# A fused four-layer kernel: which eighths of the queries keep their probabilities stationary, turned queries exchanged in pairs of chunks, and image copies issued in another stage

## The chip, the core and the metric

The kernel runs on one core of one Trainium2 chip. The metric is the device time of one execution in microseconds (us), the median of several runs. The core has a matrix engine (TensorE, PE in the profile; its weight loads are PEld), a vector engine (VectorE, DVE), an activation engine (ScalarE, ACT), a general engine (GpSimd, POOL) and an engine that only issues transfers and waits (SyncE, SP). Each of them takes its instructions in the order of the program. Data lies in 128 partitions of on-chip memory (SBUF); products are summed in eight banks (PSUM) of 512 float32 a partition. Transfers (DMA) run on 16 DMA engines, whichever queue issues them.

## The reference

Four images x of 256 channels and 64 x 64 pixels, all in float32, go through four residual layers, each on the group-normalised input (32 groups). Cut to what matters here:

```python
# layer 0: convolution 3x3, group norm, ReLU, then softmax attention over all 4096 pixels
xs  = relu(group_norm(conv3x3(_gn(x)), 8 groups))
f   = einsum('bnc,bcm->bnm', theta(xs), phi(xs))        # 4096 x 4096 logits an image
y   = einsum('bnm,bmc->bnc', softmax(f, axis=-1), g(xs))
x   = x + group_norm(conv1x1(y)) * 0.1 + xs

# layer 1: linear attention, 4 heads of 32
q, k, v = split(conv1x1(rmsnorm(_gn(x))))
q = softmax(q, over the 32 of a head);  k = softmax(k, over pixels)
context = einsum('bhdn,bhen->bhde', k, v)
x = x + rmsnorm(conv1x1(einsum('bhde,bhdn->bhen', context, q * scale)))

# layer 2: a 3x3 depthwise and a 1x1 kernel generated from the pooled image
x = x + conv1x1(depthwise3x3(_gn(x), dk), pk) + bias

# layer 3: a 1x1 kernel mixed of four experts
x = x + einsum('boc,bchw->bohw', w_mixed, _gn(x))
```

## The kernel before

**Two streams of work in one program.** The order of every engine's instructions is written out by hand. The softmax attention of batch b (`attend`) is a generator that advances by *steps*. Beside it runs a *chain* (`Chain`) of the other layers' work: layers 0's end, 1, 2 and 3 of batch b-1 (`tail`), and then the convolution of batch b+1 (`convolve`). `run` (L2271) takes a step of the chain and then one of the attention, in turns. The chain yields numbers: `yield n` lets n times `rate` steps of attention pass before its next instructions are emitted, and `yield None` exactly one. The rate is 0.785 beside batches 1 and 2 and 1.14 beside batch 3 (L2297, L2306). So a time in the program is a place in the sequence of steps, and where the chain's work comes late, the attention behind it in the same queue waits too.

**Attention.** The 4096 queries of a batch are eight *eighths* q of 512 (`NQ`), and an eighth is 16 steps m of 256 keys (`NM`); a batch has 128 steps. A step (L1207 on) issues the logits of the next step, two products of 512 columns into two banks `pf` and their exponentials by ScalarE into one tile `pr` (L1105, L1106), and then multiplies this step's probabilities with g, in one of two ways. *Moving* (L1221): g is the stationary operand, the 512 probabilities stream through, and the result `py` has channels in the partitions; the sum of the probabilities is made by VectorE, one addition of 128 x 1024 into `tot` a step (L1225, L1227). *Stationary* (L1218): 128 probabilities at a time are the stationary operand and g with a column of ones, 129 columns, streams through, so that PE makes the sum too; eight short products a step instead of two long ones. `across(q)` (L1201) chooses: stationary for q7 of every batch, and in batches 1 and 2 for every q from `TURNED` = 2 on.

**The end of an eighth** is a generator that gets one turn in each following step. For a stationary eighth, `ended` (L1166): VectorE copies the sums out of `py`, takes the reciprocal and scales; one step later PE turns the result (`ps_yt`), one more later it projects it (`ps_wy`). For a moving eighth, `ended_by_dram` (L1127): VectorE joins the halves of `tot` into `inv`, which goes to DRAM (`sum_d`, SyncE); one step later the *gather* `inv<-sum_d` (L1138, ScalarE's queue) reads it back turned, in pieces of 16 bytes; six steps after that VectorE reduces it (`r_inv`, L1142), the reciprocals go to DRAM (`rec_d`) and come back to all partitions, VectorE multiplies (`yq`), and PE projects (`ps_wy`) some 14 steps after the eighth's end.

**Linear attention in the tail** (L1520 to L1561) goes over eight chunks c of 512 pixels. A chunk is normalised (`normed`, into `xg`), turned in blocks of 32 by VectorE (`corners`), written to DRAM by four DMAs (`sent`, `turned_d`) and read back with pixels in the partitions (`fetched`), two chunks ahead of its use. ScalarE and GpSimd make the lengths (`lengths`, `rinv`), VectorE scales (`unit`). Then PE multiplies (`ps_qk`), ScalarE takes the exponentials (`qk_of`), VectorE normalises q, and a chunk later PE adds to the context (`ps_ctx`). The queries themselves are turned by the same exchange: `q_corners` (L1415), four DMAs `q_sent` of 64 KB into `q_d` and one `q_fetched` into `qT`. All of these DMAs are on SyncE. For c = 0, 2, 4 and 6 `copy_x` (L1542) also issues two DMAs of 512 KB from DRAM to DRAM there, which copy the image of batch b+2 into `xs_d`, where the layer's result is later added up; it does so in the tails that run beside attention 1 and 2.

The `outputs` of layer 1 go through a third exchange, `z_sent` and `z_fetched` through `z_d`, into the image by `z_added` with statistics (L1702 to L1723). At its end stands a chain of small steps: the statistics of the last chunk (`mv`), a product `pm`, small VectorE operations, a product `pv` (`group_finish`, L400), after which layer 2 begins.

**The depthwise stage** (`in_order`, L1920) goes over eight parts n (four chunks of 1024 pixels by two halves of the channels): ScalarE makes the centre tap, VectorE adds the eight others, one instruction of about 128 x 1024 a tap, and PE multiplies with the generated kernel (`ps_pw`). The convolution of the next batch follows, with filters of 256 KB loaded by SyncE.

**Buffers.** Tiles named by `k4` (4 KB a partition) share nine places: `pr`, `tot`, `wt`, `xg`, `qk`, `z`, `dw` and others. `k2` tiles have four places; `q_turn` is one of them before the change. A tile's instruction waits until the former tile in its place has been read for the last time.

Of the kernel before, what the change touches and what calls it, by code (L numbers as in the profile page):

```python
# [8 lines left out]
F32 = mybir.dt.float32  # L9
# [4 lines left out]
P = 128  # L14
# [3 lines left out]
CH = 1024  # L18
# [6 lines left out]
NQ = N // 512  # L25
# [11 lines left out]
TX1, MX1 = 4, 2  # L37
IX1 = HW // MX1
RW = MX * (IX + 1)
TURNED = 2  # L40
TW = 4 * (NH * 32 + 1)
US_A_STEP = 4.35
EASED = 0.68
# [61 lines left out]
def conv_preact_fast(ctx: ExitStack, tc: tile.TileContext, guard, in_range, x, wc, wtpg, ww, wqkv, wout, w1cat, wd2,  # L105
# [3 lines left out]
    nc = tc.nc  # L109
    B = x.shape[0]  # L110
# [9 lines left out]
    def k4(name):  # L120
        return k4_wide(name)[:, 0:CH]
# [3 lines left out]
    def k2(name):  # L125
        return wk.tile([P, 512], F32, tag="k2", name=name, bufs=4)
# [31 lines left out]
    qT = x_cols[:, 0, :]  # L158
# [101 lines left out]
    rows_d = tc.dram_tile([TY, P, NH, 3, NH * P], F32, name="rows_d")  # L260
    filters = tc.dram_tile([TY, P, TX - 2, NH, NH * P], F32, name="filters")
    turned_d = tc.dram_tile([NQ, 4, 32, 4, 4 * (NH * 32 + 1)], F32, name="turned_d")
    q_d = tc.dram_tile([NQ, 4, 32, 4, P], F32, name="q_d")
    z_d = tc.dram_tile([NQ, 4, 32, 4, NH * P], F32, name="z_d")
    taps = wc_s.rearrange("p h (i j) o -> p h i (j o)", i=3)

# [514 lines left out]
    def copy_x(b, part=None):  # L781
        for h in range(NH):
            cols = slice(0, N) if part is None else bass.ts(part, CH)
            nc.sync.dma_start(out=xs_d[b, h, :, cols], in_=x[b, bass.ts(h, P), cols])
# [287 lines left out]
    def attend(b):  # L1072
# [127 lines left out]

        def across(q):  # L1201

            return q == NQ - 1 or 0 < b < B - 1 and q >= TURNED

        xc = None
        logits(0)
        for i in range(NQ * NM):  # L1207
            q, m = divmod(i, NM)
# [147 lines left out]
    def linear_attention(w, b, big, qT, k4, st, sh, sums):  # L1356
# [14 lines left out]
        NC = N // 512  # L1371
# [20 lines left out]
        def sent(c, s):  # L1392
            for a in range(4):
                nc.sync.dma_start(out=turned_d[c, :, :, a, :].rearrange("c e n -> e c n"),
                                  in_=s[bass.ts(a, 32), :].rearrange("p (c n) -> p c n", c=4))
# [16 lines left out]
            for j in range(4):  # L1412
                nc.vector.tensor_scalar(x[:, :, j, 0:NH * 32], x[:, :, j, 0:NH * 32], rinv[:, j:j + 1], None, ALU.mult)

        def q_corners(qk):  # L1415
            s = k2("q_turn")
            nc.vector.transpose(s.rearrange("p (a j e) -> p a j e", a=4, j=4),
                                qk[:, :, 0:HID].rearrange("p j (a r) -> p a j r", a=4))
            return s

        def q_sent(c, s):
            for k in range(4):
                nc.sync.dma_start(out=q_d[c, :, :, k, :].rearrange("a r n -> r a n"),
                                  in_=s[bass.ts(k, 32), :].rearrange("p (a n) -> p a n", a=4))

        def q_fetched(c):
            nc.sync.dma_start(out=qT[:, bass.ts(c, 512)], in_=q_d[c].rearrange("a r c n -> (a r) (c n)"))

        def turned(xg):

# [30 lines left out]
        def qk_of(xg, rinv, first=()):  # L1461


            qk = k4("qk").rearrange("p (j o) -> p j o", j=4)
            for j in range(4):
                ps = first[j] if j < len(first) else product(xg, j)
                nc.scalar.activation(qk[:, j, :], ps[:, 0:2 * HID], AF.Exp, scale=rinv[:, j:j + 1])
                yield 0.125

            q = qk[:, :, 0:HID].rearrange("p j (g d) -> p j g d", d=HD)  # L1470
            qs = sp.tile([P, 4, HEADS], F32, name="qs", bufs=3)
            nc.vector.tensor_reduce(qs, q, AX.X, ALU.add)
            nc.vector.reciprocal(qs, qs)
            tt(q, q, qs.unsqueeze(3).to_broadcast([P, 4, HEADS, HD]), ALU.mult)
            return qk
# [12 lines left out]
        if alone:  # L1488
            w.fill(1)
            warm(3)  # L1490
            w.settle()
            xg, first = normed(0), ()
            rinv, banks = turned(xg)
            first = [product(xg, j) for j in range(2)]
            next(sums)
            xt = tokens(rinv, banks)
            yield 1
            last = None
            for c in range(NC):
                if c + 1 < NC:  # L1500
                    ahead = normed(c + 1)
                next(sums, None)
                if c == 2:
                    checks.append(counted())
                if c in (2, 4, 5):
                    next(checks[0])
                yield 0.5
                this = (yield from qk_of(xg, rinv, first)), xt
                first = ()
                if c + 1 < NC:  # L1510
                    xg = ahead
                    rinv, banks = turned(xg)
                if last is not None:
                    context(c - 1, *last)
                if c + 1 < NC:
                    xt = tokens(rinv, banks)
                last = this
            yield 1
            context(NC - 1, *last)
        else:  # L1520
            w.settle()
            nc.gpsimd.memset(quarters[3].rearrange("p (k o) -> p k o", k=16)[:, :, NH * 32:TW // 4], 1.0)
            xgs = {0: normed(0)}
            s = corners(xgs[0])
            yield 0.5
            sent(0, s)
            xgs[1] = normed(1)
            s = corners(xgs[1])
            yield 0.5
            xs = {0: fetched(0)}  # L1530
            sent(1, s)
            yield 1
            rinv = lengths(xs[0])
            last, turn = None, None
            for c in range(NC):
                if c + 1 < NC:
                    xs[c + 1] = fetched(c + 1)
                if c + 2 < NC:
                    xgs[c + 2] = normed(c + 2)
                    s = corners(xgs[c + 2])  # L1540
                unit(xs[c], rinv)
                if b + 2 < B and c % 2 == 0:  # L1542
                    copy_x(b + 2, c // 2)
                yield 0.5
                if turn is not None:
                    q_sent(c - 1, turn)
                if c + 2 < NC:
                    sent(c + 2, s)
                qk = yield from qk_of(xgs.pop(c), rinv)
                turn = q_corners(qk)  # L1550
                if c > 0:
                    q_fetched(c - 1)
                if last is not None:
                    context(c - 1, *last)
                if c + 1 < NC:
                    rinv = lengths(xs[c + 1])
                last = qk, xs.pop(c)
            q_sent(NC - 1, turn)
            yield 1
            q_fetched(NC - 1)  # L1560
            context(NC - 1, *last)  # L1561
        w.fill(1)
        rk = sp.tile([P, 1], F32, name="rk", bufs=1)
# [138 lines left out]
        s, zts = None, {}  # L1702
        for c in range(NC):
# [9 lines left out]
            s = z_corners(scaled(*zb))  # L1713
# [2 lines left out]
                w.fill(1)  # L1716
            yield 0.7
        z_sent(NC - 1, s)
        yield 0.5
        zts[NC - 1] = z_fetched(NC - 1)  # L1720
        z_added(NC - 2, zts.pop(NC - 2))
        yield 1.2
        z_added(NC - 1, zts.pop(NC - 1))  # L1723
        if b + 2 < B:
            nc.gpsimd.memset(ra[:, :, :, 0:1], 0.0)
# [39 lines left out]
    def generated(w, b, big, k4, st, sh, diag):  # L1765
# [55 lines left out]
        for c in range(N // 512):  # L1821
            if c < NC3:
                hidden(c)
            h, q = c % 2, c // 2
# [38 lines left out]
        def centre(i):  # L1863
            c, h = PARTS[i]
            t = k4("dw")
            k = h * 9 + 4
            nc.scalar.activation(t.rearrange("p (y x) -> p y x", x=HW), xin[:, h, bass.ts(c, rows), :], AF.Copy, scale=dk[:, k:k + 1])  # L1867
            return t
# [31 lines left out]
        def taps(i, some=TAPS, over=slice(0, CH // HW)):  # L1900

            c, h = PARTS[i]
            dst = dw[i].rearrange("p (y x) -> p y x", x=HW)[:, over, :]
            for ty, tx in some:
                dx = tx - 1
                x0, x1 = max(0, -dx), min(HW, HW - dx)
                k = h * 9 + 3 * ty + tx
                y = c * rows + ty
                stt(dst[:, :, x0:x1], xp[:, h, y + over.start:y + over.stop, x0 + dx:x1 + dx], dk[:, k:k + 1],
                    dst[:, :, x0:x1], ALU.mult, ALU.add)  # L1910
                yield 0.66
# [8 lines left out]
        def in_order(mine):  # L1920

            dw[mine[0]] = centre(mine[0])
            slices = [load_wp2(0), load_wp2(1)]
            for n, i in enumerate(mine):
                if n + 1 < len(mine):
                    dw[mine[n + 1]] = centre(mine[n + 1])
                for wait in taps(i):
                    yield wait * (EASED if n > 1 and b < B - 2 else 1)
                if n == 0:
                    for j in range(R):  # L1930
                        mix_kernel(slices, [j])
                        if j % 2 == 1 and j // 2 + 2 < R // 2:
                            slices.append(load_wp2(j // 2 + 2))
                        yield 0.35
                c, h = PARTS[i]
                if h == NH - 1:
                    d = [dw[2 * c + h] for h in range(NH)]
                    for s in range(2):
                        w.later(1 + s, lambda c=c, s=s, d=d: pointwise(c, s, d))
            yield 2  # L1940
            yield from w.pending()
# [950 lines left out]
```

## Time and profile before

| | |
|---|---|
| median of 3 runs | 2997.34 us (2995.27 to 2999.57) |
| time of the profiled execution | 2996.91 us |
| its span, first to last instruction | 2995.0 us |
| mean granted TensorE clock | 0.989 |
| first convolution and projections, until attention begins | 181 us |
| attention of batch 0, with the convolution of batch 1 and the projections | 181 to 744 us |
| batch 1 | 744 to 1477 us |
| batch 2 | 1477 to 2210 us |
| batch 3, and the last tail alone | 2210 to 2995 us |

The batches' borders are the starts of their first `pf` products. Batches 1 and 2 are the ones that the change of the eighths and of the copies concerns; their tails belong to the images of batches 0 and 1. Beside the attention of batch 3 runs the tail of batch 2, with neither.

How to read the profile's rows: a window row gives start and end, the length, then for each engine its busy time with the number of instructions in parentheses, the granted clock as a share, the share of the DMA engines' time in use, and GB/s. A row of waits says which instruction of which engine stood idle for whom: the total, how many times, and the longest. A timeline row gives start, length, engine and line, operation, the tile written and those read, how many in a row, and in brackets the idle time before it and what ended that. A product in float32 is listed as two records, so four `pf` records are the two products of a step.

### The profile page before, as it was taken

What the parts mean: (1) busy time and instruction counts of PE and PEld (TensorE: products, weight loads), DVE (VectorE), ACT (ScalarE), POOL (GpSimd) and SP (SyncE); (2) the same over time, 40 slices, a digit from 0 to 9 for tenths busy, and PEclk for the clock granted to TensorE, in tenths of its full rate; (3) what the DMA queues carried; (4) which work ended last, traced back from release to release, by engine and by line L of the source; (5) the groups of instructions that cost most, each with busy time, mean ns of one, the idle gap of its engine ahead of it and who ended that gap; (6) DMA issues with size and microseconds to landing.
All of it is one profiled execution on the core that took longest, in us unless ns stands there. A gap on an engine that the chain in (4) does not pass through costs nothing. (4 is left out here: it accounts for less than half of the span.)

```text
span 2995.0 us, 31153 instructions
## 1 busy us (share of the span) xinstructions
PE 2885.3 (96%) x11158; PEld 1734.3 (58%) x11158; DVE 1849.4 (62%) x2939; ACT 1341.5 (45%) x2720; POOL 189.8 (6%) x218
## 2 busy tenths in 40 slices
PE   7999999999987999999998899999999999999999
PEld 3554555566554666777555466677755644446744
DVE  8737667751656672686265585377536587783585
ACT  2234333435544543324564544422555555433674
POOL 0000000001001000000101000000000110000143
PEclk9999999999999999999999999999999999999999
DMA  5235543224565121110566502211165553225112
GB/s 226 76 84 123 65 74 68 39 32 99 169 150 134 46 78 64 53 57 32 123 191 135 113 29 78 74 50 64 32 159 122 98 126 63 25 32 135 48 65 77
DMA packets 423140, 262.71 MB, mean 88 GB/s; under 512 B 311425, under 2 KB 358273, under 8 KB 419457
## 3 DMA queue, kind: packets, MB, share of 16 engines
q1 hardware_dynamic: 123168, 239.14, 24.7%
q10 hardware_dynamic: 295200, 4.72, 7.8%
q0 software_dynamic: 4608, 16.78, 3.6%
q8 instruction: 90, 1.47, 0.2%
q14 instruction: 74, 0.60, 0.1%
HBM read 162.84 MB, written 114.53 MB: 93 GB/s over the span
## 5 line engine op out<-in xcount | busy, mean ns | idle before, releaser
L1106 ACT ACTIVATE pr<-pf 128x512 f32<-128x512 f32 x1024 | 599.1, 596 | 903.0 <-PE pf L1105 880.7
L1105 PE MATMUL pf<-tpg 128*128 128x512 f32 x2048 | 972.9, 597 | 3.9 <-ACT pr L1106 2.2
L1105 PEld LDWEIGHTS pf<-tpg 128*128 128x128 f32 x2048 | 376.5, 191 | 370.4 <-issue 339.4
L1221 PE MATMUL py<-pr,tpg 128*128 128x512 f32 x1152 | 543.7, 594 | 2.3 <-ACT pr L1106 2.3
L1218 PEld LDWEIGHTS py<-tpg,pr 128*128 128x128 f32 x3584 | 436.4, 192 | 109.1 <-issue 100.8
L1218 PE MATMUL py<-tpg,pr 128*128 128x129 f32 x3584 | 437.5, 275 | 2.4 <-ACT pr L1106 2.4
L1221 PEld LDWEIGHTS py<-pr,tpg 128*128 128x128 f32 x1152 | 219.1, 190 | 280.5 <-issue 263.7
L138 DVE TENSOR_TENSOR tot<-tot,pr 128x1024 f32<-128x1024 f32 x252 | 306.8, 1217 | 94.7 <-ACT pr L1106 94.1
L141 DVE SCALAR_TENSOR_TENSOR dw<-xp,dk,dw 128x1008 f32<-128x1008 f32 x192 | 242.2, 1269 | 7.3 <-ACT dw L1867 3.7
L706 PE MATMUL ps_conv<-v,u 128*128 128x256 f32 x864 | 195.7, 379 | 6.4 <-DVE v L138 3.6
L706 PEld LDWEIGHTS ps_conv<-v,u 128*128 128x128 f32 x864 | 161.5, 190 | 35.8 <-issue 11.5
L233 POOL TENSOR_TENSOR rstd<-rstd,half 128x2 f32<-128x2 f32 x24 | 17.7, 736 | 1933.9 <-DVE rstd L431 1789.7
L1457 PE MATMUL ps_qk<-wqkv_s,xg 128*128 128x256 f32 x496 | 116.6, 386 | 8.0 <-ACT pr L1106 7.4
L1029 PE MATMUL ps_tp<-big,wtpg_s 128*128 128x512 f32 x256 | 116.8, 595 | 4.0 <-ACT big L805 4.0
L138 DVE TENSOR_TENSOR tpg<-ps_g,bg_s 128x512 f32<-128x512 f32 x32 | 22.1, 691 | 155.7 <-PE ps_g L1034 155.7
L1457 PEld LDWEIGHTS ps_qk<-wqkv_s,xg 128*128 128x128 f32 x496 | 95.4, 194 | 32.1 <-ACT pr L1106 9.0
L141 DVE SCALAR_TENSOR_TENSOR sums<-ps_conv,sums 128x512 f32<-128x512 f32 x72 | 49.7, 690 | 90.6 <-PE ps_conv L706 84.9
L1875 PE MATMUL ps_pw<-dw,pk 128*128 128x512 f32 x192 | 86.3, 592 | 0.0
L1171 DVE COPY total<-py 128x2 f32<-128x2 f32 x28 | 4.5, 159 | 127.7 <-PE py L1218 127.7
L1029 PEld LDWEIGHTS ps_tp<-big,wtpg_s 128*128 128x128 f32 x256 | 45.9, 190 | 53.4 <-issue 42.1
L1030 ACT ACTIVATE tpg<-ps_tp,btp_s 128x512 f32<-128x512 f32 x64 | 44.0, 687 | 70.9 <-PE ps_tp L1029 70.9
L1034 PEld LDWEIGHTS ps_g<-wtpg_s,big 128*128 128x128 f32 x512 | 62.2, 192 | 15.3 <-issue 15.3
(486 smaller groups left out, 3284.4 us busy)
## 6 DMA issues: line engine op xcount, KB each, us to landing
u<-filters SPq DMA_DIRECT2D x72, 256.0 KB, 2.5
xp<-in_x_dram SPq DMA_DIRECT2D x16, 1024.0 KB, 8.4
xs_d<-big POOLq DMA_DIRECT2D x32, 512.0 KB, 6.1
wy_d<-wt SPq DMA_DIRECT2D x32, 512.0 KB, 3.0
wy<-wy_d SPq DMA_DIRECT2D x32, 512.0 KB, 5.0
out_dram<-res SPq DMA_DIRECT2D x64, 256.0 KB, 2.0
turned_d<-rt SPq DMA_DIRECT2D x96, 130.0 KB, 2.7
xs_d<-in_x_dram SPq DMA_DIRECT2D x24, 512.0 KB, 6.6
```

The costliest lines, as they stand in the source:

```text
L138: nc.vector.tensor_tensor(o, a, b, op)
L141: nc.vector.scalar_tensor_tensor(o, a, s, b, op0, op1)
L706: nc.tensor.matmul(ps[:, bass.ts(oh, IY * IX)], u[i][:, h, bass.ts(oh, P)], v[:, i, bass.ts(h, IY * IX)], start=(h == 0), stop=(h == NH - 1))
L1029: nc.tensor.matmul(ps, wtpg_s[:, h, k, :], big[:, h, cols], start=(h == 0), stop=(h == NH - 1))
L1030: nc.scalar.activation(tpg[:, k, cols], ps, AF.Identity, bias=btp_s[:, k:k + 1])
L1034: nc.tensor.matmul(ps[:, j, :], big[:, h, bass.ts(4 * c + j, P)], wtpg_s[:, h, 2, :], start=(h == 0), stop=(h == NH - 1))
L1105: nc.tensor.matmul(pf, phi[:, bass.ts(2 * m + s, P)], theta[:, bass.ts(q, 512)], start=True, stop=True)
L1106: nc.scalar.activation(pr[:, bass.ts(s, 512)], pf, AF.Exp)
L1218: nc.tensor.matmul(py[t // 2][:, t % 2, :], probs[i][:, s * 512 + t * P:s * 512 + (t + 1) * P], g[:, 2 * m + s, :], start=(begin and t % 2 ...
L1221: nc.tensor.matmul(py, g[:, 2 * m + s, 0:P], probs[i][:, bass.ts(s, 512)], start=begin, stop=end)
L1457: nc.tensor.matmul(ps[:, 0:2 * HID], xg[:, h, bass.ts(j, P)], wqkv_s[:, h, 0:2 * HID], start=(h == 0), stop=(h == NH - 1))
L1875: nc.tensor.matmul(ps, pk[:, h * NH * P + oh * P:h * NH * P + (oh + 1) * P], dw[h][:, bass.ts(s, 512)], start=(h == 0), stop=(h == NH - 1))
```

## The change

`TURNED` becomes a list of eighths, (0, 1, 3, 5, 6): in batches 1 and 2 the eighths q0 and q1 become stationary, and q2 and q4 moving. q7 stays stationary, batches 0 and 3 keep their choice.

The turned queries are exchanged in pairs of chunks. `q_turn` is now a `k4` tile for two chunks; after two chunks four DMAs of 128 KB write them to `q_d`, in a layout in which the pair's columns lie together for each partition, and one DMA reads 1024 columns back. In the chunk's order `sent(c + 2)` now stands ahead of `q_sent`, a pair is sent in the even chunk after it, and fetched in the odd one, ahead of `qk_of`.

`copy_x` leaves linear attention and is issued in the depthwise stage, at parts n = 2 to 5, one quarter of the image each.

Three yields change: after the last chunk `yield 1` becomes 0.3 ahead of the last `q_sent` and 0.7 after it; at the end of the z exchange 0.5 becomes 0.7, and 1.2 becomes 1.6.

```diff
-TURNED = 2
+TURNED = (0, 1, 3, 5, 6)
...
-    q_d = tc.dram_tile([NQ, 4, 32, 4, P], F32, name="q_d")
+    q_d = tc.dram_tile([NQ // 2, 4, 32, 2, 4, P], F32, name="q_d")
...
-            return q == NQ - 1 or 0 < b < B - 1 and q >= TURNED
+            return q == NQ - 1 or 0 < b < B - 1 and q in TURNED
...
-        def q_corners(qk):
-            s = k2("q_turn")
-            nc.vector.transpose(s.rearrange("p (a j e) -> p a j e", a=4, j=4),
+        def q_corners(c, qk, s):
+            nc.vector.transpose(s[:, bass.ts(c % 2, 512)].rearrange("p (a j e) -> p a j e", a=4, j=4),
                                 qk[:, :, 0:HID].rearrange("p j (a r) -> p a j r", a=4))
-            return s
-
-        def q_sent(c, s):
+
+        def q_sent(i, s):
             for k in range(4):
-                nc.sync.dma_start(out=q_d[c, :, :, k, :].rearrange("a r n -> r a n"),
-                                  in_=s[bass.ts(k, 32), :].rearrange("p (a n) -> p a n", a=4))
-
-        def q_fetched(c):
-            nc.sync.dma_start(out=qT[:, bass.ts(c, 512)], in_=q_d[c].rearrange("a r c n -> (a r) (c n)"))
+                nc.sync.dma_start(out=q_d[i, :, :, :, k, :].rearrange("a r i n -> r i a n"),
+                                  in_=s[bass.ts(k, 32), :].rearrange("p (i a n) -> p i a n", i=2, a=4))
+
+        def q_fetched(i):
+            nc.sync.dma_start(out=qT[:, bass.ts(i, CH)], in_=q_d[i].rearrange("a r i c n -> (a r) (i c n)"))
...
                 unit(xs[c], rinv)
-                if b + 2 < B and c % 2 == 0:
-                    copy_x(b + 2, c // 2)
                 yield 0.5
-                if turn is not None:
-                    q_sent(c - 1, turn)
                 if c + 2 < NC:
                     sent(c + 2, s)
+                if c % 2 == 0:
+                    if c > 0:
+                        q_sent(c // 2 - 1, turn)
+                    turn = k4("q_turn")
+                elif c > 1:
+                    q_fetched(c // 2 - 1)
                 qk = yield from qk_of(xgs.pop(c), rinv)
-                turn = q_corners(qk)
-                if c > 0:
-                    q_fetched(c - 1)
+                q_corners(c, qk, turn)
...
-            q_sent(NC - 1, turn)
-            yield 1
-            q_fetched(NC - 1)
+            yield 0.3
+            q_sent(NC // 2 - 1, turn)
+            yield 0.7
+            q_fetched(NC // 2 - 1)
             context(NC - 1, *last)
...
         z_sent(NC - 1, s)
-        yield 0.5
+        yield 0.7
         zts[NC - 1] = z_fetched(NC - 1)
         z_added(NC - 2, zts.pop(NC - 2))
-        yield 1.2
+        yield 1.6
         z_added(NC - 1, zts.pop(NC - 1))
...
                 if n + 1 < len(mine):
                     dw[mine[n + 1]] = centre(mine[n + 1])
+                if b + 2 < B and 2 <= n < 6:
+                    copy_x(b + 2, n - 2)
                 for wait in taps(i):
```

## The prediction

> **What bounds the kernel.** All times are in us. I read busy shares first, then the attention eighth by eighth, then what TensorE (PE) waited for.
>
> ```profile
> PE 2885.3 (96%) x11158; PEld 1734.3 (58%) x11158; DVE 1849.4 (62%) x2939; ACT 1341.5 (45%) x2720; POOL 189.8 (6%) x218
> ```
>
> PE is the bound; a change can win only where PE waits or runs slowly. The windows below are the eighths q1 to q4 of batch 1, then q1 of batch 3 (length, then busy time of PE, PEld, DVE, ACT, POOL; granted clock; DMA share and GB/s).
>
> ```profile
> 813.90:932.70 118.80, 105.62 (x342) 64.82 (x342) 76.02 (x137) 62.88 (x187) 16.34 (x13) 0.96 0.66 169
> 932.70:1012.80 80.10, 66.55 (x364) 44.10 (x363) 40.31 (x69) 37.69 (x66) 2.80 (x5) 0.91 0.39 80
> 1012.80:1088.10 75.30, 75.30 (x370) 49.51 (x369) 61.41 (x67) 32.40 (x59) 0.00 (x0) 1.00 0.02 8
> 1088.10:1186.70 98.60, 98.60 (x436) 60.85 (x435) 34.32 (x77) 38.47 (x71) 0.69 (x1) 1.00 0.29 107
> ...
> 2264.00:2367.10 103.10, 100.93 (x332) 62.54 (x331) 65.51 (x133) 55.18 (x139) 10.05 (x10) 0.98 0.62 142
> ```
>
> PE idles in q1 and q2, not in q3 and q4, where DMA is nearly or mostly free. PE's waits in q0 to q2 of batch 1:
>
> ```profile
> PE pm L413 <- DVE mv L138: 13.6, 1, 13.6
> PE ps_ctx L1485 <- DVE qk L138: 9.6, 2, 8.5
> PE ps_qk L1457 <- ACT pr L1106: 3.9, 2, 2.7
> ```
>
> To count slow running too, I price PE's work from PE's timeline: a 512-column product starts 0.86 after the last, so an attention step with moving probabilities takes 3.43, and one with stationary ones 3.50 (two `pf` starts, 939.61 and 943.11).
>
> ```profile
> 939.61 1.88 PE L1105 MATMUL pf<-tpg 128*128 128x512 f32 x4
> ...
> 943.11 1.88 PE L1105 MATMUL pf<-tpg 128*128 128x512 f32 x4
> ...
> 960.33 0.58 PE L413 MATMUL pm<-mv,avg 128*128 128x2 f32 x2 [13.55 <-DVE mv L138]
> 960.77 3.76 PE L1105 MATMUL pf<-tpg 128*128 128x512 f32 x4
> ```
>
> q1 of batch 1 holds 16 steps (54.9), 40 `ps_qk` of 256 columns (17.1), 28 `ps_ctx` (12.2), 32 `ps_o` (13.7), 2 `ps_wy` (1.7) and 0.6 of small products: 100.2. It took 118.8, so **18.6 is lost**. In the same way q2 is 56.0 + 1.7 + 5.6 (`ps_h`, from its step's 9.1) = 63.3 of 80.1, **16.8 lost**, and q0 loses 4.9. Together 40 in batch 1, and 8.1 + 15.8 + 16.7 = 41 in batch 2. Batch 3 passes the same stages (windows from 2210.3) with 0.8 + 5.4 + 0.7 = 7 lost. It copies no image, and its gathers of 16-byte pieces fall elsewhere, though its tail is also paced more gently (rate 1.14 against 0.785).
>
> **Where the 40 come from.** SyncE's timeline, then two kinds of DMA with KB and median time to landing:
>
> ```profile
> 836.63 1.14 SPq L784 DMA_DIRECT2D xs_d<-in_x_dram  x2
> 837.81 14.20 SPq L1423 DMA_DIRECT2D q_d<-q_turn  x4
> 852.11 1.86 SPq L1394 DMA_DIRECT2D turned_d<-rt  x4
> ...
> xs_d<-in_x_dram SPq DMA_DIRECT2D x24, 512.0 KB, 6.6
> ...
> inv<-sum_d ACTq DMA_DIRECT2D x18, 256.0 KB, 12.1
> ```
>
> Four `q_d` issues normally take 1.9. Here they took 14.2, because SyncE stood until the gather `inv<-sum_d` of q0, issued at 835.13, landed at 850.70. Chunk 4's exchange came that much late and PE waited 8.5. From one `turned_d` fetch to the next, a chunk with two image copies takes 10 to 11, one with neither copies nor gather 6.6 to 6.8, the one with copies and gather 19.9. PE's own work a chunk is 3.41 (`ps_qk`) + 1.73 (`ps_ctx`) + 0.785 steps (2.7) = 7.8. So copies and gather make the exchange slower than PE; without them it is faster. The second gather, of q1, is issued at 941.89 and lands at 957.11; under it the last `z_d` stores take 5.0 to 5.6 instead of 2.0 to 2.4 and the last fetch 5.8 instead of 3.4. That is the wait of 13.6.
>
> **The change part by part.**
>
> *Which eighths are stationary.* Six before and six after, so PE's 0.07 a step, the transposes and the `ps_wy` balance. In q0 and q1 VectorE loses 32 `tot` additions of 1.22, and both gathers leave. Linear attention (the steps from q0's 14 to q1's 3) has lost some 18 and gets back 14: from the chunk times, 9 of gather and four times some 3 of copies are taken out, until PE's 7.8 holds, and the first exchange's start (2.7) and about 1.5 remain. The last z: stores and fetch at their usual 2.3 and 3.4 bring `mv` about 5 sooner, VectorE without `tot` and `inv` (it is full from 930 to 943) about 2.5 more, and PE has q1's `ps_yt` and `ps_wy` (2.2) earlier to do: 13.6 - 9.7 = about 4.
>
> *The longer yields* (0.6 in all, 0.785 steps each) put another half step on average, 1.7, ahead of `pm`: about 2.5 is left. Late next is the same fetch. Cost at the other end: the chain ends at q7's step 14 or 15, so half a step may uncover a ReLU there, 0 to 3.5; I take 1.
>
> Here a rule is weighed. After the wait the granted clock reads:
>
> ```profile
> 957.00:961.00 4.00, 0.67 (x3) 0.67 (x4) 3.22 (x8) 0.00 (x0) 0.21 (x2) 0.50 0.00 1
> 961.00:966.60 5.60, 5.60 (x23) 3.53 (x23) 0.59 (x4) 1.19 (x2) 0.00 (x0) 0.64 0.00 0
> ```
>
> and the next step takes 5.8 instead of 3.5. The Trainium skill (TensorE: Matmul & The Clock Gate, "What's actually happening") says that an idle window of some 3.4 us halves the clock. By the idle row alone z gains 11; by the rule a rest under 3.4 gains the slow step's 2.3 as well, a rest of 4 nothing of it. My rest of 2.5 is near the edge: I take 12 with the small stalls at `ps_o`.
>
> *The eighths that become moving, q2 and q4.* VectorE gets 32 times 1.22. Five or so steps of each fall where it works at 3.4 of 3.5 (q2 from step 10, q4 to step 4), 13 in all; the rest in steps where it is idle (q2 steps 4 to 9, q4 steps 5 to 15). Over the depthwise stage (990 to 1111) it has some 20 of slack, and it no longer waits for PE at q3's start (2.4). Bounds 0 and 13; nearest the row of slack, I take 3, at `ps_pw`. `ended(q0)` now makes it wait for PE in linear attention, nearest row that 2.1 + 0.3: 1. In the convolution `r_inv` (1.07) meets a full VectorE: 1.
>
> *The gathers in q3 and q5.* Queued behind them: in q3 `wy_d` and the copies on SyncE, in q5 filter loads whose first two are ahead of it. `r_inv` blocks VectorE if the gather is late, but it is issued seven steps later, about 33.
>
> *The copies* (8 of 512 KB, issued in q3 and q4) leave linear attention and are covered by q3's free DMA. A rule speaks against this: the skill's page DMA: Bandwidth & Descriptors ("Issuing engines are not separate DMA queues") says that all DMAs share the same 16 engines and interleave. A pair of copies lands in 7.6, so 3.7 each; four under the gather make 15.6 + 15 = 30 by the rule, against 33 until `r_inv`. By the row (15.6 beside two copies) there is room. I take 0, with 10 as the upper bound.
>
> *Pairs.* A pair saves 5 of 10 issues, 0.48 each, on SyncE: hidden once PE bounds the chunk, counted above. `q_turn` moves from the four small buffers to the nine of `k4`; in batches 1 and 2 the absent `tot` frees the place, in batch 3 it doesn't: 0 to 4 there, and fewer issues, 0 to -2; net 1.
>
> Sum: 14 + 12 - 1 - 3 - 1 - 1 = **20 in each of batches 1 and 2**, less 1 in batch 3: 39. The profiled execution's span 2995.0 becomes 2956; with the 1.9 around it (its time is 2996.9) 2958, and the median, 2997.34, is the same to 0.5. **Forecast 2957.**
>
> **Rivals.**
> - *The exchange stays the bound* at some 9 a chunk through its latencies: 8 x 1.2 more lost, 20 becomes 10.5: **2976**. For: batch 3 is gentler paced. Against: the 6.7 of clean chunks.
> - *The depthwise stage gives it back*: gather late by 10 and `tot` exposed by 6 instead of 3, 13 more a batch: **2983**. For: VectorE at 3.4 of 3.5, the 30 against 33. Against: the empty DMA of q3.
> - *Slower: `k4` runs out.* Three `xg`, two `qk`, `q_turn`, two `pr` are eight of nine, with `wt` or batch 3's `tot` nine; then an exponential waits for a `q_turn` to be sent (4 issues 1.9 and landing 2.6: 4.5). Eight chunks in three batches at 2.2 lost are 53, less 39: **3011**. It decides from 1.6 a chunk. Against: in batches 1 and 2 `tot` leaves.
> - That the change does other than it says I exclude: the tuple leaves exactly q2 and q4 moving.
>
> **How the numbers follow.** Forecast 0.66 (own range 2936 to 2972), exchange 0.13, given back 0.11, slower 0.10. Within 0.2% (6 us, about what a measurement tells from no change) falls a part of the third, 0.04; slower 0.10, faster 0.86. Low end: 81 lost less some 8 that must stay, 2925, unlikely in full; I take 2934. High end 2984, which takes in the third case.
>
> **What would show it.** `ps_ctx <- qk` under 2 and `pm <- mv` under 5 in batches 1 and 2; clock 1.00 in q1; no `inv<-sum_d` between q0 and q2 there; q3 and q4 longer by under 4 together. Wrong if q3 grows by over 10, if PE waits at `pr` in the chunks, or if chunks stay over 9.

## The result, and the profile after

The changed kernel takes **2957.35 us** (median of 4 runs, 2954.07 to 2960.28) against 2998.45 for the kernel before (4 runs, 2995.27 to 3001.07): a ratio of 0.9863, 95% interval 0.9846 to 0.988. The profiled execution has a span of 2952.2 (2995.0 before), a time of 2954.07, and a mean granted clock of 0.996 (0.989 before).

The row of busy times, after:

```profile
PE 2878.1 (97%) x11158; PEld 1730.1 (59%) x11158; DVE 1851.7 (63%) x2939; ACT 1345.7 (46%) x2720; POOL 182.8 (6%) x218
```

PE has as many instructions as before and is busy for 7 less. So some 36 of the 42.8 by which the span got shorter were idle time of PE; the other 7 go with instructions that ran at a lowered clock before. The windows of the eighths q1 to q4 of batch 1, after, in the columns of the prediction's windows:

```profile
817.00:919.60 102.60, 102.60 (x537) 80.91 (x536) 52.59 (x112) 61.91 (x181) 12.63 (x12) 1.00 0.52 146
919.60:988.90 69.30, 65.38 (x199) 29.22 (x198) 46.26 (x73) 37.68 (x66) 1.96 (x5) 0.98 0.27 84
988.90:1060.40 71.50, 71.50 (x346) 46.60 (x345) 66.78 (x73) 31.91 (x57) 0.00 (x0) 1.00 0.44 78
1060.40:1161.40 101.00, 100.99 (x265) 46.51 (x264) 55.59 (x97) 38.60 (x72) 0.69 (x1) 1.00 0.27 104
```

q1 was 118.8 long with PE busy for 105.62; now it is 102.60 and PE is busy throughout, at a granted clock of 1.00. q2 went from 80.1 to 69.3. q3 and q4 together went from 173.9 to 172.5, though VectorE in q3 is now busy for 66.78 of 71.5. PE's waits in q0 to q2 of batch 1 (total, times, longest), after:

```profile
PE pm L413 <- DVE mv L138: 3.9, 1, 3.9
PE ps_qk L1455 <- ACT pr L1106: 3.5, 1, 3.5
PE py L1218 <- ACT pr L1106: 0.2, 1, 0.2
```

The wait at `ps_ctx` (9.6) is gone, and that at `pm` is 3.9 instead of 13.6. Not everything got better. These are the windows of q7 of batch 1, first of the kernel before, then of the one after:

```profile
1359.00:1477.10 118.10, 115.59 (x599) 80.94 (x599) 47.76 (x91) 67.27 (x124) 7.66 (x9) 1.00 0.33 70
```

```profile
1328.60:1456.50 127.90, 120.98 (x613) 84.51 (x612) 55.78 (x102) 68.03 (x124) 7.65 (x9) 0.99 0.33 75
```

The eighth at the chain's end is 9.8 longer. Part of this is work that used to lie in q6 (86.3 instead of 90.9); part is new idle time.

To keep work that only moved apart from time that was lost, I price PE's work at the spacing of its records, as the prediction did (3.43 for a moving step, 3.50 for a stationary one, 5.3 for the `ps_h` of q2), and give **lost** time, length less work, for each eighth of batch 1. The figures of before agree with the prediction's to within 1.

| | q0 | q1 | q2 | q3 | q4 | q5 | q6 | q7 | sum |
|---|---|---|---|---|---|---|---|---|---|
| before | 4.0 | 18.0 | 16.5 | 0.0 | 0.8 | 2.3 | 1.6 | 3.5 | 46.8 |
| after | 6.4 | 0.4 | 6.3 | 0.0 | 0.9 | 2.3 | 0.5 | 9.9 | 26.6 |

q1 and q2 gave 27.8; q0 took back 2.4 and q7 6.4. The loss in q0 lies in its last two steps, where linear attention begins; before, 4.4 more of that start fell into the first three steps of q1, where 0.3 is left. By the starts of their first `pf`, batch 1 went from 732.9 to 712.7, batch 2 from 733.3 to 713.3, and batch 3 with the tail from 784.7 to 782.4. That is 20.2, 20.0 and 2.3.

### The profile page after: what moved, and what is told of

It reads as the page before. It is cut to its first block, busy times and chain, and to the rows that moved or that the text cites. A ratio compares the mean times of both kernels' runs of the same rounds, so it can differ in the third digit from the quotient of the medians.

```text
span 2952.2 us, 31046 instructions
## 1 busy us (share of the span) xinstructions
PE 2878.1 (97%) x11158; PEld 1730.1 (59%) x11158; DVE 1851.7 (63%) x2939; ACT 1345.7 (46%) x2720; POOL 182.8 (6%) x218
## 5 line engine op out<-in xcount | busy, mean ns | idle before, releaser
L1874 PE MATMUL ps_pw<-dw,pk 128*128 128x512 f32 x192 | 86.3, 593 | 0.0
L1122 DVE BATCH_NORM_STATS2 wy_st<-wt 128x6 f32<-128x512 f32 x64 | 42.8, 688 | 47.8 <-ACT wt L1159 33.7
L2196 ACT ACTIVATE res<-ps_ex,b 128x512 f32<-128x512 f32 x56 | 38.2, 686 | 72.6 <-PE ps_ex L2188 69.4
```

Of the source, the lines that this page charges most:

```text
L1122: nc.vector.bn_stats(st[:, h, q, :], wt[:, h, :])
L1874: nc.tensor.matmul(ps, pk[:, h * NH * P + oh * P:h * NH * P + (oh + 1) * P], dw[h][:, bass.ts(s, 512)], start=(h == 0), stop=(h == NH - 1))
```

## The experiments

Twelve kernels ran: parts of the change taken out of the kernel after, parts put alone into the kernel before, a replacement of the disputed transfer, alone and with the copies moved, and two attempts at the loss in q7. The kernels ran on three chips, and the ratio is to the kernel before on the same chip; its medians there were 2995.51 beside the four kernels with a part taken out, 2997.36 beside the eighths alone, the copies alone, the rows alone and the pause of 1.4, and 2996.32 beside the other four. So a difference of medians between kernels of two groups is good to about 3. "q1", "q2" and "q7" are lengths in batch 1, "`pm`" and "`ps_ctx`" are PE's waits there.

| kernel | median | ratio, 95% | q1 | q2 | q7 | `pm` | `ps_ctx` |
|---|---|---|---|---|---|---|---|
| before | 2998.45 | 1 | 118.7 | 80.1 | 118.0 | 13.6 | 9.6 |
| after | 2957.35 | 0.9863, 0.9846 to 0.988 | 102.7 | 69.3 | 127.9 | 3.9 | 0 |
| after, yields of z as before | 2952.69 | 0.9855, 0.9838 to 0.9871 | 102.7 | 72.2 | 118.0 | 6.6 | 0 |
| after, copies as before | 2962.54 | 0.9889, 0.9873 to 0.9906 | 104.5 | 70.9 | 128.2 | 4.3 | 0 |
| after, pairs as before | 2958.96 | 0.9875, 0.9859 to 0.9892 | 102.8 | 71.5 | 128.4 | 4.5 | 0 |
| after, eighths as before | 2976.26 | 0.9934, 0.9917 to 0.995 | 105.2 | 77.1 | 129.3 | 10.1 | 0 |
| before, new eighths | 2961.77 | 0.988, 0.9865 to 0.9895 | 106.2 | 72.8 | 118.0 | 6.5 | 0 |
| before, new place of copies | 2974.33 | 0.9926, 0.9911 to 0.9941 | 106.0 | 80.0 | 118.0 | 13.3 | 1.1 |
| before, pairs | 2989.06 | 0.9974, 0.9964 to 0.9984 | 116.6 | 79.4 | 118.0 | 13.3 | 7.9 |
| before, new yields of z | 2998.82 | 1.0009, 1.0001 to 1.0018 | 119.5 | 76.0 | 128.9 | 9.8 | 10.4 |
| before, gathers in rows | 2969.73 | 0.9912, 0.9897 to 0.9927 | 107.4 | 75.3 | 118.0 | 8.7 | 1.0 |
| before, both of copies and rows | 2959.38 | 0.9878, 0.9863 to 0.9894 | 103.3 | 75.3 | 118.0 | 9.2 | 0 |
| after, pause 1.4 | 2948.85 | 0.9841, 0.9827 to 0.9854 | 102.7 | 72.2 | 118.0 | 5.5 | 0 |
| after, pause 0.7 and yield 2.4 | 2950.07 | 0.9844, 0.9831 to 0.9857 | 102.7 | 64.3 | 136.4 | 0 | 0 |

### Parts taken out of the kernel after

**The yields of z** as before:

```diff
-        yield 0.7
+        yield 0.5
...
-        yield 1.6
+        yield 1.2
```

> The changed kernel with the two yields of the z exchange set back to 0.5 and 1.2. Theory (the longer yields push the chain's end past the attention): in batches 1 and 2 the q7 eighth takes 121 us instead of 127.9, the wait of PE at pm rises from 3.9 to about 7, with some 2 us of half clock behind it, and the time is about 2956 us, within 4 of the changed kernel. Rival (the chain's end is late because of the tot additions in q2 and q4, not because of the yields): q7 stays at 127 to 128, the wait at pm rises all the same, and the time is 2966 to 2970 us.

Measured: 2952.69. PE waits 6.6 at `pm` instead of 3.9, q2 is 2.9 longer, and q7 is back at 118.0. The lengths of batches 1 and 2 come to 712.1 and 713.7 against 712.7 and 713.3: the longer yields win some 3 at `pm` and give it all back at the chain's end. The fall of q7 and the rise at `pm` are the theory's, though the time is 3 below the theory's 2956. How they do so is read in PE's timeline there. After:

```profile
1398.84 1.95 PE L1218 MATMUL py<-tpg,pr 128*128 128x129 f32 x16
1400.62 0.28 PE L413 MATMUL pm<-mv,avg 128*128 128x2 f32 x2
1400.76 2.03 PE L1218 MATMUL py<-tpg,pr 128*128 128x129 f32 x16
1402.63 0.28 PE L429 MATMUL pv<-ev,avg 128*128 128x2 f32 x2
1403.72 0.66 PE L1183 MATMUL ps_yt<-ident,yn 128*128 128x128 f32 x4 [0.81 <-DVE yn L138]
1408.49 3.62 PE L1193 MATMUL ps_wy<-yt,ww_s 128*128 128x512 f32 x4 [4.11 <-ACT yt L1188]
```

And with the yields of z as before:

```profile
1396.01 0.28 PE L413 MATMUL pm<-mv,avg 128*128 128x2 f32 x2
...
1399.74 0.28 PE L429 MATMUL pv<-ev,avg 128*128 128x2 f32 x2
1399.88 1.96 PE L1105 MATMUL pf<-tpg 128*128 128x512 f32 x4
1401.68 1.95 PE L1218 MATMUL py<-tpg,pr 128*128 128x129 f32 x16
```

This is the group norm of the convolution: `pm`, `pv`, then the normalisation `big` on ScalarE, and the products `ps_tp` of the next batch. With the old yields, attention steps follow `pv` and cover it. With the new ones the last `py` of the batch comes before `pv`, so nothing is left: PE waits 0.8 for `yn`, and 4.1 for `yt`, a copy that stands in ScalarE's queue behind a `big` that waits for the norm:

```profile
1405.38 2.63 ACT L805 ACTIVATE big<-xp,sh,sc 128x256 f32<-128x256 f32 x4 [1.46 <-DVE sh L138]
1407.81 0.62 ACT L1188 COPY yt<-ps_yt 128x512 f32<-128x512 f32 x1
```

The two `ps_wy` products then take 3.62 instead of the 1.72 of four records at 0.43 apiece, at a granted clock that fell to about half for the 3.4 from 1408.4. 0.8 + 4.1 + 1.9 is 6.8; q7 lost 6.4 more.

**The copies** as before (the two lines back behind `unit`, the two in the depthwise stage out):

> The changed kernel with the image copies back in linear attention. Theory (copies make the exchange slower than PE): a chunk with copies takes 9 to 10 us at SyncE and q1 of batches 1 and 2 loses 4 to 8 us more, time about 2967 us. Rival (with the gather gone the copies are hidden): q1 within 1 us of 102.7, time 2957 to 2959 us.

Measured: 2962.54, 3.4 more in batch 1 and 3.7 in batch 2. q1 is longer by 1.8, between the rival's 1 and the theory's 4 to 8, and the time too lies between the two. With no gather beside them, the copies cost little; that the exchange's lead over PE takes them up is argued below.

**The eighths** as before (`TURNED = 2`, `q >= TURNED`):

> The changed kernel with q0 and q1 of batches 1 and 2 moving again and q2 and q4 stationary. Theory (the two gathers cost some 9 us in linear attention and 12 at the end of the z exchange, in each of two batches): the waits at ps_ctx and pm come back at 4 to 9 and 9 to 13 us, time 2990 to 3000 us. Rival (the copies and SyncE's number of issues were what mattered, the gather only added to them): waits under 3 and 6 us, time 2965 to 2975 us.

Measured: 2976.26, just above the rival's range and far below the theory's. Of the 13.0 that batch 1 got longer, 7.8 are in q2, where the wait at `pm` is 10.1, as the theory had it. q1 is longer by 2.5 only, with the gather of q0 back in it and no wait at `ps_ctx`, as the rival had it. So once copies and single chunks are gone, linear attention bears a gather; the theory had this wrong.

**The pairs** as before (the exchange by chunks, in the old order, with the longer yields and the new place of the copies kept):

> The changed kernel with the turned queries sent chunk by chunk again, from the small buffers, in the order of before. Theory (PE bounds the chunks once copies and gather are away, so fewer issues are worth nothing): q1 of batches 1 and 2 within 2 us of 102.7, time 2956 to 2961 us. Rival (SyncE's issues bound the exchange): q1 longer by 8 to 10 us, time about 2976 us.

Measured: 2958.96, with 715.0 and 717.0 in batches 1 and 2: 2 to 4 more a batch. By the ratios that is some 4 in all, and the intervals overlap. q1 stays within the theory's 2. Pairs are a small part.

### Parts put alone into the kernel before

**The new eighths alone** (`TURNED` and `across`, nothing else):

> The kernel of before with the choice of eighths alone changed. Theory (with the copies and twelve issues a chunk still there, the gathers cost 9 us in linear attention and 12 at the last z): PE's waits at ps_ctx fall from 9.6 to under 3 us and at pm from 13.6 to about 5; q1 about 108 us, q2 about 73; time about 2960 us. Rival (the parts only work together): q1 over 112 us, time over 2972 us.

Measured: 2961.77, which is 35.6 below the kernel before on its chip, where the whole change took 41.1. PE's waits in q0 to q2 of batch 1:

```profile
PE pm L413 <- DVE mv L138: 6.5, 1, 6.5
PE ps_qk L1457 <- ACT pr L1106: 4.6, 2, 3.4
PE pf L1105 <- ACT qk L1467: 1.9, 1, 1.9
```

`ps_ctx` is gone from the list although all eight copies are still issued among the chunks.

**The new place of the copies alone:**

```diff
-                if b + 2 < B and c % 2 == 0:
-                    copy_x(b + 2, c // 2)
...
+                if b + 2 < B and 2 <= n < 6:
+                    copy_x(b + 2, n - 2)
```

> The kernel of before with the image copies alone moved to the depthwise stage. Theory (a chunk with copies takes 10.5 us at SyncE, one without 6.7, PE needs 7.8): some 8 us less in q0 and q1 of batches 1 and 2 together, the gather's wait at ps_ctx still over 5 us, time about 2980 us. Rival (the gather alone holds the exchange): under 3 us a batch, time 2989 to 2995 us.

Measured: 2974.33. The theory expected the wait at `ps_ctx` to stay, since the gather stays. PE's waits say otherwise (a second wait at `ps_ctx`, of 0.3, stands further down the list):

```profile
PE pm L413 <- DVE mv L138: 13.3, 1, 13.3
PE ps_qk L1457 <- ACT pr L1106: 3.1, 1, 3.1
PE ps_o L1611 <- ACT z L1636: 1.1, 1, 1.1
PE ps_ctx L1485 <- issue: 0.8, 1, 0.8
```

Did SyncE stop standing at the gather, then? Its own waits, first in the kernel before, then in this one:

```profile
SPq L1423 <- DMA inv<-sum_d: 12.1, 1, 12.1
```

```profile
SPq L1423 <- DMA inv<-sum_d: 10.6, 1, 10.6
```

It stands nearly as long, and PE hardly feels it. The stall goes by VectorE: its next turning of a chunk (`corners`) waits for the late `turned_d`, and in its queue the `qk` that PE needs stands behind. First before, then in this kernel:

```profile
856.15 1.46 DVE L1388 STREAM_TRANSPOSE rt<-xg 128x512 f32<-128x512 f32 x2 [11.84 <-DMA turned_d<-rt]
```

```profile
845.73 1.46 DVE L1388 STREAM_TRANSPOSE rt<-xg 128x512 f32<-128x512 f32 x2 [8.77 <-DMA turned_d<-rt]
```

A chunk is sent and fetched two chunks ahead of its use. The pixels of chunk 4, the last that PE used before it felt the stall, had landed 10.4 before their `ps_ctx` in the kernel before, and 16.2 here. So the copies had eaten some 6 of that lead, and the gather's stall met PE nearly in full; without the copies the lead takes most of the 10.6 in. Gather and copies draw on the same reserve, so removing either repairs most of it, and their gains don't add up in full.

**Pairs alone:**

> The kernel of before with the pairs alone: q_turn for two chunks, sent and fetched in pairs, with the chunk's new order and the yields of 0.3 and 0.7 after the last. Theory (copies and gather hold the exchange; pairs take 5 of 10 issues off SyncE in two chunks and shorten the chunks with copies): waits at ps_ctx 3 to 9 us, pm's wait unchanged near 13, 3 to 8 us a batch, time about 2985 us. Rival (the tile moved to k4 makes tot, q_turn and the probabilities wait for places): new waits at pr in q0 and q1, time over 2996 us.

Measured: 2989.06, with `ps_ctx` at 7.9 and `pm` at 13.3 still there, and no new wait at `pr`.

**The yields of z alone:**

> The kernel of before with the longer yields of the z exchange alone. Theory (they trade the wait at pm for the same time at the chain's end): pm's wait falls from 13.6 by 3 to 4 us, q7 loses some 6 more, time within 4 us of before. Rival (a step put over a wait is a step won): 5 to 7 us less.

Measured: 2998.82, no gain, as the theory had it: `pm` falls from 13.6 to 9.8, and q7 is 10.9 longer, with the same 4.1 of `ps_wy <- yt`. It is the same exchange of one wait for another.

### What in the gather costs

**The gathers of q0 and q1 read in rows** in batches 1 and 2. It moves the same 256 KB in the same queue at the same place, and leaves VectorE's work as it was. The turned sums of those four eighths are not the reference's.

```diff
-            nc.scalar.dma_start(out=inv.rearrange("r (p k) -> r p k", k=4), in_=sum_d[at].rearrange("p (r k) -> r p k", k=4))
+            if 0 < b < B - 1 and q < 2:
+                nc.scalar.dma_start(out=inv, in_=sum_d[at])
+            else:
+                nc.scalar.dma_start(out=inv.rearrange("r (p k) -> r p k", k=4), in_=sum_d[at].rearrange("p (r k) -> r p k", k=4))
```

> The kernel of before, in which the gathers of q0 and q1 of batches 1 and 2 read their 256 KB in rows as they lie, not turned in pieces of 16 bytes; so for those four eighths the sums that divide the attention's result are not the reference's, and all instructions stay. VectorE keeps its tot additions in q0 and q1. Theory (the gather's small pieces are what the eighths remove): as with the eighths alone, waits at ps_ctx under 3 us and at pm about 5 to 7, time within 5 us of that kernel's. Rival (VectorE's 32 tot additions a batch matter as much): waits at ps_ctx 4 to 6 and at pm over 8 us, time over 2972 us.

Measured: 2969.73. In batch 1 the two transfers land 3.6 and 3.7 after their issue, where the gathers took 15.6 and 15.2 (in batch 2, 3.0 and 5.0 for 15.9 and 15.4). The wait at `ps_ctx` is 1.0, that at `pm`:

```profile
PE pm L413 <- DVE mv L138: 8.7, 1, 8.7
```

So 27.7 of the 34.8 by which the new eighths alone shortened the span (spans 2995.0, then 2967.3 with rows and 2960.2 with the new eighths) come from reading in rows and not in pieces. The theory's "within 5" of the eighths alone is missed all the same: the time is 8 more, and `pm` falls to 8.7 where 5 to 7 was expected. What is left, 8.7 against 6.5 at `pm` above all, goes with the other things that the eighths move: VectorE's `tot` and `inv`, and the place of the products. No run takes these apart.

**Copies moved and gathers in rows**, both edits above:

> The kernel of before with the copies moved and the four gathers of q0 and q1 of batches 1 and 2 read in rows as they lie; so for those four eighths the sums that divide the attention's result are not the reference's. Theory (copies and gather eat the same lead of two chunks, so that in linear attention either cure does nearly all, and at the last z only the gather counts): q1 of batches 1 and 2 at 105 to 106 us as with the copies alone, pm's wait 8 to 9 as with the gather alone, time about 2963 us. Rival (the two add up): q1 under 104 us and the time under 2955 us.

Measured: 2959.38. q1 is 103.3, against 106.0 by the copies and 107.4 by the rows alone: from 118.7 the two take 12.7 and 11.3 singly and 15.4 together, not 24. That is the shared reserve again, by numbers. The theory's 105 to 106 was too high and the rival's "under 104" came true, but the rival's time, under 2955, did not.

### Against the loss in q7

Between the depthwise stage and the convolution's wait for its pending products the chain pauses for `yield 2`, while the attention goes on. If the longer z yields only push the chain's end past the attention, a shorter pause should bring it back, with `pm` left alone.

```diff
-            yield 2
+            yield 1.4
```

> The changed kernel with the 2 attention steps' pause after the depthwise stage cut to 1.4, which takes back the 0.6 that the z exchange was given. Theory (the chain ends half a step too late for the last ReLUs): q7 of batches 1 and 2 falls from 127.9 to about 118 to 121 us with the work that moves, pm's wait stays at about 4; 5 to 7 us a batch, time 2943 to 2948 us on a chip where before takes 2998. Rival (the end of q7 is not set by the chain's length): within 2 us of the changed kernel, 2955 to 2959 us.

Measured: **2948.85** (5 runs, 2947.65 to 2950.18), the lowest median of all: 8.5 below the changed kernel by the medians, 6.3 by the spans (2945.9 and 2952.2). The two ratios' intervals, from two chips, still overlap by 0.0008. q7 is 118.0 again; PE's waits there:

```profile
PE py L1218 <- ACT pr L1106: 1.7, 2, 1.2
PE ps_tp L1029 <- ACT big L805: 1.3, 2, 0.7
```

`ps_wy <- yt` is gone. `pm`, at 5.5, is longer than in the kernel after, and q2 of batch 1 is at the 72.2 of the old yields again, so that win is lost there; the end is won back: 710.4 and 709.9 in batches 1 and 2, which is 2.3 and 3.4 less than in the kernel after, where the theory had 5 to 7. Against the kernel with the old yields (2952.69) little is left, some 4 by the ratios, and the intervals overlap.

**More of both**, z's last yield 1.6 to 2.4 and the pause 2 to 0.7:

> The changed kernel with 2.4 in place of 1.6 in the z exchange's last yield, and 0.7 in place of 2 after the depthwise stage. Theory (the wait at pm of about 4 to 5 us with its stretch of half clock needs one more step of attention over it, taken from a pause that nothing needs): pm's wait under 2 us, q2 of batches 1 and 2 about 67 to 68 us, time about 2943 us on a chip where before takes 2997. Rival (the pause is needed for the last pointwise products): q4 or q5 longer by 3 us or more, time 2948 to 2955 us.

Measured: 2950.07. The wait at `pm` is gone and q2 is 64.3, the best of all runs. But q7 is 136.4 with 11.5 lost, where the kernel after lost 9.9; 5.9 of them are at `ps_tp <- big`. And q5 loses 3.5 instead of 2.3. The time falls into the rival's range, but not by its way: q4 and q5 are not longer. A shorter pause doesn't pay for so long a yield: its end is late again.

## Why the prediction was right, step by step

The gain came from the place and through the mechanism that it named. That the total agrees so closely, 20 a batch against 20.2 and 20.0, is luck: 5 of forecast costs in each batch (the depthwise stage, `ended(q0)`, `r_inv`) did not come, and the chain's end cost 5.4 more than forecast.

**What bounds.** PE's idle and slow time in q1 and q2 was the thing to win: the lost time of batch 1 fell by 27.8 in those two eighths. The signs named for it came: `ps_ctx <- qk` and the gather are gone from these stages, `pm` is 3.9 and 4.4 in batches 1 and 2, and q1 has the clock at 1.00. q3 and q4 together are 1.4 shorter, where under 4 longer was allowed.

**Linear attention, 14.** From step 14 of q0 to step 3 of q1 the lost time fell from 18.6 to 5.8: 12.8. The sum was nearly right, the way to it was not. It added 9 for the gather and four times 3 for the copies, up to the limit of PE's own 7.8 a chunk. The runs show that each alone takes nearly the whole way (11.3 and 12.7 on q1). What saved the forecast was the limit, not the addends.

**The last z, 12.** The lost time there (from step 12 of q1 to step 7 of q2) fell from 18.9 to 6.3: 12.6. The first term, 5 from stores and fetch without the gather, is 4.9 (13.6 to 8.7 by the rows alone). Of 2.5 from VectorE and 2.2 from products done earlier, 2.2 came in all (8.7 to 6.5), so "about 4" was 6.5. The yields, for 1.7 forecast, brought 2.7 (6.6 to 3.9).

**The clock at `pm`.** The Trainium skill (TensorE: Matmul & The Clock Gate, "What's actually happening") puts the edge at an idle window of about 3.4; the forecast's rest of 2.5 lay below it, the measured 3.9 above, and the clock fell:

```profile
940.00:944.20 4.20, 1.10 (x4) 0.71 (x5) 4.17 (x9) 0.00 (x0) 0.00 (x0) 1.00 0.00 0
944.20:947.60 3.40, 3.40 (x5) 1.33 (x4) 1.67 (x5) 1.19 (x2) 0.00 (x0) 0.50 0.50 159
```

In these windows of the kernel after, the second starts after the idle one and runs at 0.50 for 3.4. The step behind `pm` takes 5.35 instead of 3.43, so rule and trace agree, and 1.9 of the slow step's 2.3 stayed lost. Only where `pm` waits for nothing, in the last experiment, does q2 come to 64.3.

**The chain's end, 1: the term that was mis-sized.** It measured 6.4, nearly twice the upper bound of 3.5. The prediction took half a step to uncover a ReLU behind the last attention step. It uncovers more: the group norm ahead of the ReLU, a copy queued behind it on ScalarE, and the slow clock after the wait. Against the 2.7 at `pm`, the yields were no gain: two runs show it, and the shorter pause shows what it cost.

**The depthwise stage, 3.** It measured nothing: lost time in q3 and q4 is 0.9 instead of 0.8, with VectorE at 66.78 of 71.5. The slack of 20 held all 13 of the bound.

**`ended(q0)` and `r_inv` in the convolution, 1 each.** q5 lost 2.3 as before, and the list of waits after has no `pf <- qk` such as the 1.9 that the eighths alone show while the copies are in place. In the combination both terms were 0.

**Copies under the gather, 0.** Right, on a smaller margin than thought. In q3 the gather was issued at 998.60 among four copies and landed at 1014.89; `r_inv` came at 1018.0, so there were 19.4 until it and not 33, and 3.1 to spare (2.2 in batch 2). The 30 that the prediction worked out from the Trainium skill's rule that all DMAs share the same 16 engines (DMA: Bandwidth & Descriptors, "Issuing engines are not separate DMA queues") would have made it late by 11. What the sharing cost is shown by the kernel with the copies as before, where the same gather has none beside it: it took 11.2 and 11.3 there in batches 1 and 2, against 16.3 and 17.3. Sharing cost the gather 5 to 6, not the copies' whole 15; the four copies landed within 7.5 of their issue in batch 1. So they do share, but their times don't add up, and the prediction's row, 15.6 beside two copies, was the better guide.

**Pairs, hidden.** About right: 2 to 4 a batch when taken out last, so the "0" was a little low. Batch 3 gained 2.3 where a loss of 1 was expected, and its wait for `pr` is 2.4 (2.2 before).

The rivals: that the exchange stays the bound is refuted by q1's 102.60 of 102.60; that the depthwise stage gives the gain back, by q3 and q4; that `k4` runs out, by the waits for `pr`: in batch 1 3.5 at the first `ps_qk` (3.9 before) and 0.2 at `py`, in batch 3 2.4, with no loss in pairs alone either.

Alone, the parts take 34.8 (eighths), 22.5 (copies) and 6.1 (pairs) off the span, and the yields add 1.1; that sums to 62, and together they bring 42.8. Put in first, the eighths are nearly all of it, and the other three parts add 8 by span; taken out last, they are worth 24.8 (2977.0 to 2952.2). With a shared reserve the share of a part depends on what is already there.

Why does SyncE stand for a transfer of ScalarE's queue whose data none of its instructions needs? The semaphores in the trace, which no view above prints, answer it. In this stretch the transfers of both queues signal their landing on eight semaphores in turn, in the order of the program, and an issue waits until the last transfer on its own semaphore has landed. The gather of q0 signals semaphore 104; the `q_d` issue that stood is the eighth transfer behind it, signals 104 too, and waits for 104 alone. It goes out at 850.72, the gather having landed at 850.70. With the copies moved, and with the eighths as before, the gather and the issue that stands share 109 in the same way. So the wait comes from how the program hands out its semaphores; another semaphore for the gather was not tried.

What stays open: what of the rest at `pm` is VectorE's work and what the place of the products, and why `pm` in batch 1 is longer again with the shorter pause.

## What to carry to other kernels

When a stage works ahead by a fixed lead, count what draws on that lead together: two disturbances that each seem to cost their full length are often one reserve run empty, and removing either of them gets most of the gain. A pause moved into a chain comes out at the chain's other end: look at what stands there, and whether anything still covers it, before pricing it at a fraction of a step. And before a slow transfer is moved, ask what its piece size costs.

## What the runs showed of the hardware

- In the same queue at the same places, 256 KB of DRAM to SBUF took 15.2 to 15.9 in pieces of 16 bytes and 3.0 to 5.0 in rows. In q3, with no image copies beside it, a gather in pieces took 11.2, and 16.3 with four.
- A transfer's semaphore can hold up another queue: SyncE's issue stood for 12.1 for a gather of ScalarE's queue that signals the same semaphore eight transfers earlier.
- Every stretch at half clock in the trace after lasts 3.4 (one 3.1 at the end of the span), eight in all; before there were also 6.8, 10.2 and 13.7, whole multiples of 3.4 to the rounding, and a 4.6 at the span's end.
